# A step of Newton's method moved from VectorE to GpSimd in the second of four graph layers

## The chip, the cores and the metric

The kernel runs on one core of one Trainium2 chip. The metric is the device time of one execution in microseconds (us), as the median of several runs. Besides the timed runs there is one profiled execution, from which all views of the profile come.

## The reference

Four graph layers follow each other on 4096 nodes of 256 features, with one 4096 x 4096 adjacency matrix of 0 and 1. Each layer is `x = layernorm(x + layer(x, adj))`. The change sits in the second layer, an attention of four heads under a mask:

```python
def _layernorm(x, axis=-1, eps=1e-5):
    m = jnp.mean(x, axis=axis, keepdims=True)
    v = jnp.var(x, axis=axis, keepdims=True)
    return (x - m) / jnp.sqrt(v + eps)
...
q = _split_heads(x @ Wq + bq)
k = _split_heads(x @ Wk + bk)
v = _split_heads(x @ Wv + bv)
mask = (edge.T.astype(jnp.float32) - 1.0) * 10000.0
scores = jnp.einsum('hnd,hmd->hnm', q, k) / np.sqrt(HEAD_DIM)
scores = scores + mask[None, :, :]
attn = jax.nn.softmax(scores, axis=-1)
ctx = jnp.einsum('hnm,hmd->hnd', attn, v)
```

What matters here is the layer norm at the end: for every node one value `1 / sqrt(v + eps)` is needed.

## The kernel before, in words

All features stay in SBUF, in the tile `X` (128 partitions, 32 tiles of nodes, 257 columns). Every layer works on blocks of 512 nodes, eight blocks in all, which are the columns of a tile of scores; for each block it goes over all 4096 nodes on the other side.

In the second layer (`multi_head_attention`) that other side is cut into 64 half tiles of 64 nodes. A unit is a pair of a block `b` and a half tile `j`, and there are 512 units. For each unit:

- `scores` (line 622) puts the products of keys and queries of all four heads into a PSUM tile `p`, of which there are three; ScalarE takes the exponential in place (line 624).
- `weights` (line 634) multiplies on VectorE by the mask into an SBUF tile `prob`, of which there are eight.
- The row sums of `prob` are gathered for the softmax in three slots of the tile `den`: for even `j` GpSimd adds `prob` into slot 0 (line 641; for `j` = 0 a copy, line 639); for odd `j` a DMA issued by GpSimd adds `prob` into slot 1 or 2 in turn (line 647; the first two of a block are plain DMAs of the SP queue, line 645).
- `sums` (line 655) multiplies `prob` with the values on TensorE, three units behind `scores` (`LAG = 3`).

While a block runs, the block before it is finished piece by piece by `finish(b - 1, j)`: the slots of `den` are joined on VectorE (line 664), the sums and results are turned on TensorE (lines 677 to 692), divided and added to `X` (lines 706 and 709). Mean and variance of four tiles of nodes follow at `j` = 21 to 27 (lines 125 and 126). At `j` = 29 `begin_root` adds `eps` on VectorE (line 151), and ScalarE computes a first value of the inverse root as `exp(-0.5 * ln(v))` (lines 130 and 131). `end_root` makes it exact by one step of Newton's method, four instructions on 128x4 numbers (lines 137 to 140), at `j` = 33. At `j` = 35, 37, 39 and 41 `scale_row` (line 155) writes the normalised rows. `finish` is called with the `j` that is three behind the unit whose `scores` and `weights` were just written, so that its instructions stand behind `weights` of `j` + 3.

The order on an engine is settled in two ways. In this loop it is written out by hand for TensorE, VectorE and ScalarE:

```python
fixed = {mybir.EngineType.PE, mybir.EngineType.DVE, mybir.EngineType.Activation}
with tc.manual_schedule(engines=fixed):
```

These three keep the order of the program. The order on GpSimd and on the SP queue is chosen by the framework's planner, from dependencies, its own costs, and the order of the program as priority. In the third layer only TensorE's order is by hand, in the fourth none. Waits between engines are added by the framework.

Of the kernel before, what the change touches and what calls it, by code (L numbers as in the profile page):

```python
# [14 lines left out]
OP = mybir.AluOpType  # L15
# [13 lines left out]
def kernel(  # L29
# [27 lines left out]
    nc = tc.nc  # L57
# [65 lines left out]
    def one_row(mv, k, y):  # L123
        st = fin.tile([P, 6], FP, name="bn")
        nc.vector.bn_stats(st, y)
        nc.vector.bn_aggr(mv[:, k, :], st)
# [4 lines left out]
        nc.scalar.activation(r, r, AF.Exp, scale=-0.5)  # L131
        return r

    def end_root(v, r, n):

        s = fin.tile([P, n], FP, name=f"s{n}")
        nc.vector.tensor_tensor(s, r, r, OP.mult)
        nc.vector.tensor_tensor(s, s, v, OP.mult)
        nc.vector.tensor_scalar(s, s, -0.5, 1.5, OP.mult, OP.add)  # L139
        nc.vector.tensor_tensor(r, r, s, OP.mult)  # L140

    def inverse_root(v, n):

        r = first_root(v, n)
        end_root(v, r, n)
        return r

    def begin_root(mv):
        n = mv.shape[1]
        v = fin.tile([P, n], FP, name=f"v{n}")  # L150
        nc.vector.tensor_scalar_add(v, mv[:, :, 1], EPS)
        return v, first_root(v, n), n

    def scale_row(y, mv, r, k):
        nc.vector.tensor_scalar(y, y, mv[:, k, 0:1], r[:, k:k + 1], OP.subtract, OP.mult)

    def normalise(ys, mv):
        v, r, n = begin_root(mv)
        end_root(v, r, n)
        for k, y in enumerate(ys):  # L160
            scale_row(y, mv, r, k)
# [35 lines left out]
    def additive_heads(a, H, slope, early, narrow, ahead):  # L197
# [7 lines left out]
        with ExitStack() as lay:  # L205
# [92 lines left out]
            def finish(b, j):  # L298

                if j in (4, 10):  # L300
                    k = (j - 4) // 3
                    pos[b, k], pos[b, k + 1] = turned(bank, b, k), turned(bank, b, k + 1)
                    if k == 0 and b + 2 < NB:
                        rows(b + 2, pos[b, 0][:, HC + 1, :])
                if j in (4, 7, 10, 13):
                    k = (j - 4) // 3
                    outputs(pos[b, k], b, k)
                elif j == 15:
                    roots[b] = begin_root(mvs[b])
                elif j == 18:  # L310
                    end_root(*roots[b])
                elif j in (19, 21, 23, 25):
                    k = (j - 19) // 2
                    scale_row(X[:, b * QB + k, :D], mvs[b], roots[b][1], k)
# [194 lines left out]
    def multi_head_attention(w_sb, b_sb, tail, rows_of_den, narrow_edges):  # L509
# [11 lines left out]
        kept, den, rden, mvs, roots = {}, {}, {}, {}, {}  # L521
        with ExitStack() as lay:
# [140 lines left out]
            def join_sums(b, n, eng=nc.vector):  # L663
                eng.tensor_tensor(den[b][:, 0, :], den[b][:, 0, :], den[b][:, n, :], OP.add)

            def row_sums(bank, b):


                kept[b].append(fin1.tile([P, QW], FP, name=f"kept{KC}"))
                pds = [bank() for _ in range(KC)]  # L670
                for r in range(KC):
                    for s in range(2):
                        for c in range(KC):
                            g = 2 * r + s
                            half = slice(c * d, (c + 1) * d)
                            lo = r * QW + s * QW // 2
                            nc.tensor.matmul(pds[c][g * G:(g + 1) * G, :QW // 2], ones[half, :G],
                                             den[b][half, 0, lo:lo + QW // 2], start=True, stop=True)
                for c in range(KC):
                    nc.scalar.copy(kept[b][KC][:, c * QW // 2:(c + 1) * QW // 2], pds[c][:, :QW // 2])  # L680

            def turned_row_sums(bank, b):
                pd = bank()
                for k in range(QB):
                    nc.tensor.transpose(pd[:, k * P:(k + 1) * P], kept[b][KC][:, k * P:(k + 1) * P], ident)
                return pd

            def turned_half(bank, b, k):
                po = bank().rearrange("p (k f) -> p k f", f=D)
                for i in range(2):  # L690
                    for c in range(KC):
                        nc.tensor.transpose(po[:, i, c * P:(c + 1) * P],
                                            kept[b][c][:, (k + i) * P:(k + i + 1) * P], ident)
                return po

            def reciprocals(pd, b):
                rden[b] = fin.tile([P, QB, H], FP, name="rden4")
                parts = pd.rearrange("p (c k r s g) -> p k c r s g", c=KC, k=2, r=KC, s=2)
                for s in range(2):
                    nc.vector.reciprocal(rden[b][:, 2 * s:2 * s + 2, :].rearrange("p k (c r) -> p k c r", c=KC),  # L700
                                         parts[:, :, :, :, s, 0])

            def half(po, b, k):

                heads = po.rearrange("p k (h d) -> p (k h) d", h=H)
                nc.vector.tensor_tensor(heads, heads, rden[b][:, k:k + 2, :].rearrange("p k h -> p (k h)").unsqueeze(2)
                                        .to_broadcast([P, 2 * H, d]), OP.mult)
                y = X[:, b * QB + k:b * QB + k + 2, :D]
                nc.vector.tensor_tensor(y, po, y, OP.add)

            def halves():

                p = ps.tile([P, KC, QW], FP, name="p")
                left = [p[:, r, :] for r in range(KC)]
                return lambda: left.pop(0)

            def finish(b, j):

                rows = [X[:, b * QB + k, :D] for k in range(QB)]
                if j in (7, 9):  # L720
                    join_sums(b, j // 2 - 2)
                elif j == 12:
                    row_sums(halves(), b)
                elif j == 15:
                    bank = halves()
                    pd = turned_row_sums(bank, b)
                    po = turned_half(bank, b, 0)
                    reciprocals(pd, b)
                    half(po, b, 0)
                elif j == 18:  # L730
                    half(turned_half(halves(), b, 2), b, 2)
                elif j in (21, 23, 25, 27):
                    k = (j - 21) // 2
                    if k == 0:
                        mvs[b] = fin.tile([P, QB, 2], FP, name="mv")
                    one_row(mvs[b], k, rows[k])
                elif j == 29:
                    roots[b] = begin_root(mvs[b])
                elif j == 33:
                    end_root(*roots[b])  # L740
                elif j in (35, 37, 39, 41):
                    k = (j - 35) // 2
                    scale_row(rows[k], mvs[b], roots[b][1], k)
# [6 lines left out]
            with tc.manual_schedule(engines=fixed):  # L750
                for i in range(len(units) + LAG):
                    b, j = units[i - LAG] if i >= LAG else (-1, 0)
                    if i < len(units):
                        scores(*units[i])
                    if j == NH - 1:
                        sums(b, j)
                    if i < len(units):
                        weights(*units[i])
                    if b >= 0 and j < NH - 1:
                        sums(b, j)  # L760
                    if b > 0:
                        finish(b - 1, j)
# [238 lines left out]
```

## Time and profile before

| What | Value |
|---|---|
| Median of 3 runs | 2920.45 us (2920.34 to 2920.62) |
| Profiled execution, its own time | 2920.01 us |
| Its span, first to last instruction | 2918.1 us |
| Granted TensorE clock | 0.999 |
| Busy: TensorE, VectorE, ScalarE, GpSimd | 2901.0, 1959.0, 1668.3, 927.0 us |
| Second layer's loop | from about 815 to 1723 us of the span |
| In it: busy TensorE, VectorE, ScalarE, GpSimd | 902.4, 705.2, 566.7, 802.2 us of 908 us |

PE is TensorE's matmul, PEld its load of weights, DVE is VectorE, ACT is ScalarE, POOL is GpSimd, SP is SyncE. L139 is line 139 of the kernel. [...] An arrow in brackets names what ended an idle time.

### The profile page before, as it was taken

Reading aid. Unit: us, or ns where it says so; the run is one execution under the profiler, and the core shown is the slowest. Engines: PE = TensorE matmul, PEld = TensorE weight load, DVE = VectorE, ACT = ScalarE, POOL = GpSimd, SP = SyncE. Lnnn points to the kernel's source line nnn. Section 1 sums busy time; section 2 is a strip of 40 time slices with the busy share of each in tenths; the row PEclk is TensorE's granted clock in tenths of the full one; section 3 lists DMA queues with packets and bytes.
Section 4 is the critical chain, followed back from the end, with each engine's and each line's share of the span. In section 5 each row is a group of like instructions: output and inputs, shape, how many; then the busy total and the mean of one; then the engine's idle time right before and its main releaser. Section 6 shows DMA issues by size and latency. Waiting matters only on the chain.

```text
span 2918.1 us, 50377 instructions
## 1 busy us (share of the span) xinstructions
PE 2901.0 (99%) x20269; PEld 1564.5 (54%) x20269; DVE 1959.0 (67%) x2545; ACT 1668.3 (57%) x2613; POOL 927.0 (32%) x647
## 2 busy tenths in 40 slices
PE   9999999999999999999999999999999999999998
PEld 5333333333643333333333358888888777777776
DVE  8899999997677877877877765555655323333333
ACT  7899999997356666666666654444454222222222
POOL 0010010100068888988889860000000000000000
PEclk9999999999999999999999999999999999999999
DMA  7566666664068888889889874444442333333331
GB/s 204 107 135 140 136 140 142 135 134 84 1 142 191 182 187 189 181 186 191 180 189 188 184 164 138 153 152 150 154 136 60 49 58 58 58 58 58 58 58 29
DMA packets 207148, 374.94 MB, mean 128 GB/s; under 512 B 15057, under 2 KB 90817, under 8 KB 206018
## 3 DMA queue, kind: packets, MB, share of 16 engines
q0 software_dynamic: 102304, 177.77, 38.5%
q1 hardware_dynamic: 104336, 193.69, 20.2%
q8 instruction: 159, 2.61, 0.3%
q14 instruction: 75, 0.61, 0.1%
q10 hardware_dynamic: 274, 0.26, 0.0%
HBM read 317.07 MB, written 21.04 MB: 116 GB/s over the span
## 4 chain that ended last, share of the span: by engine, by line
PE 97%; DVE 2%; ACT 0%; issue 0%; DMA 0%; DVEq 0%; SPq 0%
PE acc L274 23%; PE acc L875 15%; PE p L622 15%; PE acc L655 14%; PE acc L440 8%; PE g L440 8%; PE p L864 4%; PE g L864 3%; PE g L550 2%; PE g L177 1%; PE pv L564 1%; PE g L118 1%; PE acc L823 1%; PE acc L177 1%; DVE prob L634 1%; DVE s L139 1%
## 5 line engine op out<-in xcount | busy, mean ns | idle before, releaser
L634 DVE TENSOR_TENSOR prob<-p,mask 128x1024 f32<-128x1024 f32 x512 | 623.0, 1223 | 197.2 <-ACT p L624 193.4
L624 ACT ACTIVATE p<-p,shift 128x1024 f32<-128x1024 f32 x512 | 556.2, 1088 | 331.9 <-PE p L622 331.0
L274 PE MATMUL acc<-prob,V 128*32 128x512 f32 x6144 | 664.0, 592 | 1.2 <-DVE prob L264 1.2
L641 POOL TENSOR_TENSOR den<-den,prob 128x1024 f32<-128x1024 f32 x248 | 618.8, 2495 | 72.4 <-DVE prob L634 62.9
L261 ACT ACTIVATE prob<-row,dst 128x512 f32<-128x512 f32 x1020 | 633.2, 712 | 0.1
L264 DVE SCALAR_TENSOR_TENSOR prob<-prob,mask 128x2048 f32<-128x2048 f32 x256 | 582.7, 2288 | 24.1 <-ACT prob L261 20.4
L622 PE MATMUL p<-qT,kT 64*64 64x512 f32 x4096 | 532.7, 590 | 5.6 <-DVE prob L634 5.6
L655 PE MATMUL acc<-prob,V 64*64 64x512 f32 x4096 | 531.5, 589 | 0.0
L875 PE MATMUL acc<-X,prob 128*128 128x257 f32 x2048 | 485.2, 380 | 0.0
L875 PEld LDWEIGHTS acc<-X,prob 128*128 128x128 f32 x2048 | 388.5, 190 | 160.7 <-issue 113.4
L868 DVE TENSOR_TENSOR prob<-prob,mask 128x512 f32<-128x512 f32 x256 | 176.5, 691 | 418.8 <-ACT prob L867 417.6
L274 PEld LDWEIGHTS acc<-prob,V 128*32 128x32 f32 x6144 | 197.3, 110 | 453.1 <-issue 434.2
L91 POOL COPY tick<-prob 128x1 f32<-128x1 f32 x35 | 39.8, 1136 | 1017.5 <-DVE prob L264 644.3
L432 ACT ACTIVATE e<-row,dst 128x512 f32<-128x512 f32 x256 | 184.2, 722 | 235.1 <-DVE prob L434 209.0
L655 PEld LDWEIGHTS acc<-prob,V 64*64 64x64 f32 x4096 | 155.9, 133 | 285.3 <-issue 278.1
L622 PEld LDWEIGHTS p<-qT,kT 64*64 64x64 f32 x4096 | 153.7, 133 | 284.4 <-issue 255.7
L434 DVE SCALAR_TENSOR_TENSOR prob<-e,mask 128x512 f32<-128x512 f32 x256 | 178.5, 698 | 185.7 <-PE acc L440 94.5
L808 POOL DMA_DIRECT2D mask<-in_adjT x64 | 47.5, 743 | 633.8 <-DVE prob L868 509.7
L647 POOL DMA_DIRECT2D den<-prob x240 | 225.9, 941 | 28.0 <-DVE prob L634 21.0
L867 ACT ACTIVATE prob<-p 128x512 f32<-128x512 f32 x144 | 85.8, 596 | 260.1 <-PE p L864 246.0
L440 PE MATMUL g<-V,prob 128*128 128x257 f32 x1024 | 225.6, 380 | 0.0
L440 PE MATMUL acc<-V,prob 128*128 128x257 f32 x1024 | 225.1, 380 | 0.0
(154 smaller groups left out, 1972.2 us busy)
## 6 DMA issues: line engine op xcount, KB each, us to landing
mask<-in_adjT SPq DMA_DIRECT2D x256, 512.0 KB
den<-prob POOLq DMA_DIRECT2D x240, 512.0 KB, 5.3
mask<-edges SPq DMA_DIRECT2D x256, 128.0 KB
mask<-in_adjT POOLq DMA_DIRECT2D x64, 512.0 KB, 5.6
edges<-in_adj POOLq DMA_DIRECT2D x32, 512.0 KB, 9.8
den<-prob SPq DMA_DIRECT2D x16, 512.0 KB
row<-far SPq DMA_DIRECT2D x7, 1024.0 KB
X<-in_x SPq DMA_DIRECT2D x7, 512.0 KB
```

The costliest lines, as they stand in the source:

```text
L261: nc.scalar.activation(z[:, h, :], r, AF.Relu, bias=-1.0, scale=dst[:, j, h:h + 1])
L264: nc.vector.scalar_tensor_tensor(z, z, 1.0, mask[m][:, j % MJ, :].unsqueeze(1).to_broadcast([P, H, QW]), OP.add, OP.mult)
L274: nc.tensor.matmul(acc[b][h * G:(h + 1) * G, n, :], part, prob[b, j][:, h, :], start=(j == 0), stop=(j == NT - 1))
L440: nc.tensor.matmul(acc[b][k][:, :D + 1], prob[b, j][:, k * P:(k + 1) * P], V[:, j, :], start=(j == 0), stop=(j == NT - 1))
L622: nc.tensor.matmul(p[c * d:(c + 1) * d, r, :], kT[half, c, j * d:(j + 1) * d], qT[half, c, cols], start=True, stop=True)
L624: nc.scalar.activation(p, p, AF.Exp, bias=shift)
L634: nc.vector.tensor_tensor(z, p, mask[m][:, j % MJ, :].unsqueeze(1).to_broadcast([P, KC, QW]), OP.mult)
L641: nc.gpsimd.tensor_tensor(to, to, flat, OP.add)
L647: nc.gpsimd.dma_start(to, flat, accum_op=OP.add)
L655: nc.tensor.matmul(acc[b][c][r * d:(r + 1) * d, :], V[half, j, r * d:(r + 1) * d], prob[b, j][half, r, :], start=(j == 0), stop=(j == NH - 1))
L864: nc.tensor.matmul(p, T[:, 0, j * P:(j + 1) * P], T[:, 1, cols], start=True, stop=True)
L875: nc.tensor.matmul(acc[b][k], prob[b, j][:, k * P:(k + 1) * P], X[:, j, :], start=(j == 0), stop=(j == NT - 1))
```

## The change

In the second layer's `finish`, the four instructions of `end_root` are issued on GpSimd rather than on VectorE, and at half tile 31 of the running block rather than at 33. `end_root` gets the engine as an argument; its other callers keep VectorE. `begin_root` stays at 29, `scale_row` at 35 to 41.

```diff
-    def end_root(v, r, n):
+    def end_root(v, r, n, eng=nc.vector):
 
         s = fin.tile([P, n], FP, name=f"s{n}")
-        nc.vector.tensor_tensor(s, r, r, OP.mult)
-        nc.vector.tensor_tensor(s, s, v, OP.mult)
-        nc.vector.tensor_scalar(s, s, -0.5, 1.5, OP.mult, OP.add)
-        nc.vector.tensor_tensor(r, r, s, OP.mult)
+        eng.tensor_tensor(s, r, r, OP.mult)
+        eng.tensor_tensor(s, s, v, OP.mult)
+        eng.tensor_scalar(s, s, -0.5, 1.5, OP.mult, OP.add)
+        eng.tensor_tensor(r, r, s, OP.mult)
...
                 elif j == 29:
                     roots[b] = begin_root(mvs[b])
-                elif j == 33:
-                    end_root(*roots[b])
+                elif j == 31:
+
+                    end_root(*roots[b], nc.gpsimd)
                 elif j in (35, 37, 39, 41):
```

## The prediction

> **What bounds the kernel now.** I read the page's chain that ended last first. It says that the whole program is a stream of matmuls:
>
> ```profile
> PE 97%; DVE 2%; ACT 0%; issue 0%; DMA 0%; DVEq 0%; SPq 0%
> ```
>
> So only what opens a gap on TensorE (PE) costs time, and a step on VectorE (DVE) or GpSimd (POOL) counts only where it makes PE late. Next, the waits of the second layer alone (815 to 1725 us). Columns: who waited on whom, total us, times, longest.
>
> ```profile
> PE p L622 <- DVE prob L634: 5.6, 8, 0.8
> POOL den L641 <- DVE prob L634: 62.9, 121, 3.1
> ```
>
> PE waits eight times here: once at the layer's start (819 us), and seven times for a late product of line 634. The loop calls `finish(b - 1, j)` in seven blocks, so that is once per block. The chain in order of time shows what made line 634 late (start us, length us):
>
> ```profile
> 1216.34 0.90 PE p L622 x8
> ...
> 1218.44 1.22 DVE prob L634
> ...
> 1219.97 2.54 DVE s L139
> ...
> 1222.61 1.23 DVE prob L634
> ...
> 1223.89 1.09 PE p L622 x8
> ```
>
> Line 139 is one instruction of the very step that the change moves, on 128x4 numbers. The two answers for line 139 (layer two and the boundary after it, then the first layer; min/median/max ns) show how odd its 2.5 us are:
>
> ```profile
> L139 DVE TENSOR_SCALAR s<-s x8: 170/2528/2528, 992.6 to 1761.0; 128x4 f32<-128x4 f32 x8
> L139 DVE TENSOR_SCALAR s<-s x8: 170/170/171, 183.1 to 745.7; 128x4 f32<-128x4 f32 x8
> ```
>
> The same instruction costs 0.17 us where GpSimd isn't adding. In layer two it costs 2.51 to 2.53 us in all seven blocks. The timeline gives the reason:
>
> ```profile
> 1216.87 2.36 POOL L641 TENSOR_TENSOR den<-den,prob 128x1024 f32<-128x1024 f32 x1
> ...
> 1219.19 0.87 POOL L647 DMA_DIRECT2D den<-prob  x1
> ...
> 1219.82 2.63 POOL L641 TENSOR_TENSOR den<-den,prob 128x1024 f32<-128x1024 f32 x1
> ...
> 1219.97 2.53 DVE L139 TENSOR_SCALAR s<-s 128x4 f32<-128x4 f32 x1
> 1222.53 0.16 DVE L140 TENSOR_TENSOR r<-r,s 128x4 f32<-128x4 f32 x1
> 1222.61 2.35 DVE L634 TENSOR_TENSOR prob<-p,mask 128x1024 f32<-128x1024 f32 x2
> ...
> 1224.13 0.87 POOL L647 DMA_DIRECT2D den<-prob  x1 [1.67 <-DVE prob L634]
> ```
>
> GpSimd's add starts at 1219.82, line 139 at 1219.97; the add ends at 1222.45, line 139 at 1222.50. The small instruction sits out the whole add. Line 634 of the next half tile waits behind it, and both PE and GpSimd (1.67 us idle) wait for that.
>
> [...] The trace agrees: line 139 ends 0.05 us after the add. It also shows what isn't held: line 155, a TENSOR_SCALAR whose scalars come from SBUF, stays at 404 to 424 ns everywhere, and line 634 (one input in PSUM) at about 1.22 us beside running adds.
>
> **The cost of the stall.** The timeline of PE alternates lines 622 and 655 every 0.858 us. Around the stall the starts are 1222.17, 1223.89, 1224.80, 1225.65: three steps take 3.48 us in place of 3 x 0.858 = 2.575 us. The loss is 0.905 us; the other six blocks show the same 1.71 or 1.72 us step. Seven blocks: 7 x 0.905 = **6.3 us**. PE loses less than DVE: the product of half tile 37 starts at 1222.61, while its undisturbed place is 1218.44 + 1.717 = 1220.16, so it is 2.45 us late. PE thus had 2.45 - 0.905 = 1.55 us of cushion.
>
> **The change part by part.**
>
> *Removed from DVE:* lines 137 to 140 at half tile 33 of the finished block. They come when half tile 36 of the running block is on DVE (the loop runs three ahead); I call the times by that count. From 1219.58 to 1222.61 they hold DVE 3.03 us per block; the line 634 that follows goes back to 1220.16. Worth 0.905 us of PE per block. Nothing else on PE waits for line 634 in these blocks, so I name no next late thing.
>
> *Unchanged:* line 151 and the two ACT instructions of `begin_root`, at half tile 32. ACT's wait there (1.42 us) costs PE nothing now and will not then. Their result is there at 1213.35.
>
> *Added to POOL:* four instructions on 128x4, in program order after the add of half tile 34 (1216.87 to 1219.2) and ahead of the DMA issue of half tile 35. No trace row has such an instruction. The nearest is the tick copy on one element a partition:
>
> ```profile
> L91 POOL COPY tick<-prob x35: 185/314/2519, 31.7 to 2186.0; 128x1 f32<-128x1 f32 x35
> ```
>
> Below, 0.185 us each; above, its mean of 1.136 us. The long ones belong to the first layer, beside line 264, a 2.29 us DVE instruction with both inputs in SBUF, and none such runs at half tile 34. [...] I take 0.3 us each, 1.2 us in all (0.74 to 4.5).
>
> *Moved past:* the DMA issue of half tile 35 goes from 1219.19 to 1220.4, the add of 36 from 1219.82 to about 1221.0. That add ends at about 1223.4, where today the next issue starts at 1224.13: the 1.67 us idle pays for the 1.2 us. The issue lands 5.3 us later (median), at 1225.7; its source buffer is wanted again eight half tiles on, by line 634 of 43 at about 1220.16 + 6 x 1.717 = 1230.5; and the next addition into the same slot is issued at 39, near 1227. Both are covered, and with 4.5 us (landing at 1229.0) the buffer still is. SP's queue isn't passed, and no DMA is added. Cost to PE: none.
>
> *Added wait:* line 155 on DVE (half tile 38, after line 634 ends at 1221.88 + 1.22 = 1223.1) now waits for POOL. The roots are ready at 1219.2 + 1.2 = 1220.4, 2.7 us before. At 1.136 us each they come at 1223.7; DVE waits 0.6 us, and line 634 of half tile 39, queued behind, is late by about that, within the cushion of 1.55. So the price doesn't touch PE up to (1223.1 + 1.55 - 1219.2) / 4 = 1.36 us each.
>
> **Sum:** 2920.01 - 6.3 = 2913.7 us for the profiled execution (span 2918.1 and 1.9 around it). The median of the runs is 0.44 above it, so **2914.1 us**, 0.22% faster. A measurement of this kernel can tell about 0.2% (5.8 us) from no change, so the whole gain just reaches it.
>
> **The rivals.**
>
> *Dear instructions (same).* If each costs 1.5 us with the hand-over between dependent ones, the roots come at 1225.2, DVE waits 2.1, PE loses 2.1 - 1.55 = 0.55 per block: 7 x (0.905 - 0.55) = 2.5 gained, 2918 us. [...] Against: the two starts on POOL in the first microsecond, a fill of `ident` and the select on it, lie 0.28 us apart.
>
> *POOL's queue (slower).* Line 749 fixes the order of PE, DVE and ACT alone; POOL's is the planner's. If it puts the four behind the add of half tile 38, that add waits for 1223.1, ends near 1225.5, and the roots come at 1226.7. DVE waits 3.6, PE loses 3.6 - 1.55 = 2.05 per block: 7 x (2.05 - 0.905) = 8 us slower, 2928 us. Behind the add of 36 they come at about 1223.4 and cost nothing, so it decides between 36 and 38. For: nothing ties the four to place. Against: POOL's adds and issues stand in program order today, and where the planner orders DVE too (1760 us) lines 137 to 140 stand together.
>
> *The stall stays (same).* If the lock is not the cause, or another DVE instruction meets it, 2920. Against: the seven identical lock-outs, and that none of lines 155, 125 and 634 beside an add is long.
>
> *The planner moves later work (either way).* Layers three and four leave DVE and ACT to it; moved times could change orders there by some us, 2911 to 2918.
>
> **How the numbers follow.** Forecast 0.70, dear 0.07, queue 0.09, stays 0.06, later work 0.08. Of the forecast I count a seventh as ending just inside 0.2%. Faster: 0.60 + 0.06 of the last rival = 0.66. Slower: 0.09. Same: the rest, 0.25. The forecast's own range is 2913.2 to 2915; to hold eight in ten it reaches up over the dear case, 2918, and down to 2912.8 for a little from later work.
>
> **What would show it.** Right: no line 139 on DVE in layer two; four small POOL instructions once per block, together, about 1.2 us; PE's step of 1.72 us gone, the total of PE waiting for line 634 down from 5.6 to about 0.8; DVE not waiting ahead of line 155; the block's period 113.70 - 0.9 = 112.8 us. Wrong: an idle time on DVE ended by POOL, or a block of 113.7 us.

## The result and the profile after

The changed kernel takes 2913.39 us (median of 13 runs, 2912.29 to 2914.40); the kernel before took 2920.01 us in the runs beside it (13 runs, 2918.88 to 2920.95). That is 6.6 us less, a ratio of 0.9978 (95% interval 0.9969 to 0.9986). The forecast was 6.3 us less.

The profiled execution went from 2920.01 to 2912.32 us, 7.7 us less. To see where, read the first and last start of a line that opens and closes the second layer: the answer for line 622 on PE (min/median/max ns, first and last start in us). First before, then after:

```profile
L622 PE MATMUL p<-qT,kT x4096: 589/589/640, 815.7 to 1718.7; 64*64 64x512 f32 x196
```

```profile
L622 PE MATMUL p<-qT,kT x4096: 589/589/640, 814.5 to 1711.1; 64*64 64x512 f32 x196
```

The stretch shrinks from 903.0 to 896.6 us, by 6.4. The other 1.2 us lie ahead of the layer, where the two kernels do the same; behind it nothing was gained or lost by more than 0.3 us (line 875, now 876, last starts at 2909.7 and 2902.4). So the layer is the place to compare kernels in, and I call 896.6 and 903.0 the *length of the stretch* below.

In the page's chain of the changed kernel VectorE has 1% in place of 2%, and of PE's waits for line 634 in the second layer only the one at the layer's start is left:

```profile
PE 99%; DVE 1%; ACT 0%; DMA 0%; issue 0%; SPq 0%; DVEq 0%
```

```profile
PE p L622 <- DVE prob L634: 0.8, 1, 0.8
```

The timeline of the changed kernel shows GpSimd and the two VectorE instructions that hand over to and take from it (start us, length us):

```profile
1209.76 0.16 DVE L151 TENSOR_SCALAR v<-mv 128x4 f32<-128x4 f32 x1
1210.00 2.36 POOL L641 TENSOR_TENSOR den<-den,prob 128x1024 f32<-128x1024 f32 x1
...
1212.33 0.19 POOL L137 TENSOR_TENSOR s<-r 128x4 f32<-128x4 f32 x1
1212.60 0.20 POOL L138 TENSOR_TENSOR s<-s,v 128x4 f32<-128x4 f32 x1
1212.89 0.19 POOL L139 TENSOR_SCALAR s<-s 128x4 f32<-128x4 f32 x1
...
1213.16 0.20 POOL L140 TENSOR_TENSOR r<-r,s 128x4 f32<-128x4 f32 x1
1213.63 0.88 POOL L647 DMA_DIRECT2D den<-prob  x1 [0.27 <-issue]
...
1220.07 0.41 DVE L155 TENSOR_SCALAR X<-X,mv,r 128x256 f32<-128x256 f32 x1
```

The four start 0.27 to 0.29 us apart and hold back the next DMA issue to 1.30 us after the first of them. They stand behind the add of half tile 32, the first one after line 151, not behind that of 34. The roots are there at 1213.4, 6.7 us before line 155 wants them.

### The profile page after: what moved, and what is told of

Same layout as the page of the kernel before. It is cut to its first block, busy times and chain, and to the rows that moved or that the text cites. A ratio compares the mean times of both kernels' runs of the same rounds, so it can differ in the third digit from the quotient of the medians.

```text
span 2910.5 us, 50377 instructions
## 1 busy us (share of the span) xinstructions
PE 2898.3 (100%) x20269; PEld 1564.1 (54%) x20269; DVE 1940.4 (67%) x2517; ACT 1668.1 (57%) x2613; POOL 932.3 (32%) x675
## 4 chain that ended last, share of the span: by engine, by line
PE 99%; DVE 1%; ACT 0%; DMA 0%; issue 0%; SPq 0%; DVEq 0%
PE acc L274 23%; PE acc L876 15%; PE acc L655 15%; PE p L622 15%; PE g L440 8%; PE acc L440 8%; PE p L865 4%; PE g L865 3%; PE g L550 2%; PE g L177 1%; PE pv L564 1%; PE g L118 1%; PE acc L824 1%; PE acc L177 1%; PE g L286 0%; PE p L692 0%
## 5 line engine op out<-in xcount | busy, mean ns | idle before, releaser
L641 POOL TENSOR_TENSOR den<-den,prob 128x1024 f32<-128x1024 f32 x248 | 628.6, 2535 | 71.3 <-DVE prob L634 64.4
L647 POOL DMA_DIRECT2D den<-prob x240 | 233.4, 972 | 15.8 <-DVE prob L634 7.5
```

The source lines that it names most:

```text
L641: nc.gpsimd.tensor_tensor(to, to, flat, OP.add)
L647: nc.gpsimd.dma_start(to, flat, accum_op=OP.add)
```

## The experiments

All ratios are against the kernel before, in the same session on the same chip.

### e1: the half tile alone

```diff
-                elif j == 33:
+                elif j == 31:
                     end_root(*roots[b])
```

> The four instructions stay on VectorE and only move from half tile 33 to 31, so that they stand behind line 634 of half tile 34, which ends when GpSimd starts its add of the same half tile. Lock theory: line 139 sits out that add as well, DVE is some 2.6 us late for half tile 35, the cushion of 1.55 us takes part of it and PE loses about 1.1 us in each of seven blocks: 1.4 us more than before, about 2921.5 (2920 to 2923), line 139 again near 2 us or more. Rival, the slot is what pays and the engine only goes along: 2913.5, line 139 at 0.17 us.

Measured: 2921.52 us, ratio 1.0006 (0.9997 to 1.0014); the stretch is 904.4 us, 1.4 longer than before. Line 139 in this kernel:

```profile
L139 DVE TENSOR_SCALAR s<-s x7: 2236/2241/2241, 990.2 to 1673.5; 128x4 f32<-128x4 f32 x7
```

It sits out the add of half tile 34 in place of that of 36: in one block the add runs from 1217.81 to 1220.16, line 139 from 1217.95 to 1220.19. "Lock" in the recorded texts is to be read as this hold, an instruction on VectorE that ends only when the add does (0.03 us after it here). The earlier half tile brings nothing on VectorE; that the medians show 1.3 us more is what was forecast, but the interval does not tell it from no change.

### e2: another form of line 139

```diff
-    def end_root(v, r, n):
+    halves_ = const.tile([P, 2], FP, name="nwt")
+    nc.vector.memset(halves_[:, :1], -0.5)
+    nc.vector.memset(halves_[:, 1:], 1.5)
+
+    def end_root(v, r, n, minus=-0.5, plus=1.5):
...
-        nc.vector.tensor_scalar(s, s, -0.5, 1.5, OP.mult, OP.add)
+        nc.vector.tensor_scalar(s, s, minus, plus, OP.mult, OP.add)
...
-                    end_root(*roots[b])
+                    end_root(*roots[b], halves_[:, :1], halves_[:, 1:])
```

> As before (VectorE, half tile 33), but line 139 of the second layer takes its two constants from SBUF, one per partition, as line 155 does, so that it is no longer a form which the add holds up. Rival A, [...]line 139 falls to 0.17 us, nothing takes its place, the gain is the change's own, 2913.5. My theory, with a lock that also holds an instruction with two SBUF inputs beside a GpSimd instruction that reads SBUF: line 139 falls to 0.17 us, but line 140 (two SBUF inputs), right behind it, sits out the rest of the add at 2.2 to 2.4 us, and the time stays at 2920 (2919 to 2921).

Measured: 2919.96 us, ratio 0.9999 (0.9991 to 1.0007), as I expected, but not for my reason. The timeline, where lines 141 to 144 are the four (143 is line 139 of before) and 645 is GpSimd's add:

```profile
1218.46 0.16 DVE L142 TENSOR_TENSOR s<-s,v 128x4 f32<-128x4 f32 x1
1218.52 2.60 POOL L645 TENSOR_TENSOR den<-den,prob 128x1024 f32<-128x1024 f32 x1
1218.66 2.49 DVE L143 TENSOR_SCALAR s<-s,nwt 128x4 f32<-128x4 f32 x1
1221.19 0.16 DVE L144 TENSOR_TENSOR r<-r,s 128x4 f32<-128x4 f32 x1
```

The instruction with its constants in SBUF is held just as long (2.49 us, 2.53 before), and the hold did not move to the line behind it (0.16 us). Line 155 has that form too, so the prediction's remark that it isn't held is in doubt. The probe below (e8) takes that up.

### e3: the four behind the add of half tile 38

```diff
-                        nc.gpsimd.tensor_tensor(to, to, flat, OP.add)
+                        added[b, j] = nc.gpsimd.tensor_tensor(to, to, flat, OP.add)
...
-                elif j == 31:
-                    end_root(*roots[b], nc.gpsimd)
                 elif j in (35, 37, 39, 41):
                     k = (j - 35) // 2
+                    if k == 0:
+                        seen = added[b + 1, 38]
+                        with tc.issue_after(getattr(seen, "ins", seen)):
+                            end_root(*roots[b], nc.gpsimd)
```

> The changed kernel with the four GpSimd instructions tied behind the add of half tile 38 of the running block (line 155 still stands behind line 634 of 38 on VectorE). Theory of the cushion: the add of 38 starts when its product is there, some 0.1 us after line 155 could start, takes 2.4 us, the four 1.1 us: line 155 waits 3.6 to 3.8 us, PE loses that less 1.55, about 2.1 to 2.2 per block, 7 x 2.15 = 15 us over the changed kernel: 2928 (2926 to 2931). Rival, PE has more slack than one block's reading showed: 2913 to 2920. Rival, no cushion: 7 x 3.7 = 26 us, 2939.

Measured: 2927.36 us, ratio 1.0026 (1.0016 to 1.0036): slower than before. The waits of the second layer (who, on whom: total us, times, longest):

```profile
DVE X L155 <- POOL r L140: 25.5, 7, 3.7
PE p L622 <- DVE prob L634: 12.9, 8, 1.8
```

VectorE waits 25.5 / 7 = 3.64 us per block. Against the changed kernel the time is 2927.36 - 2913.39 = 14.0 us longer, 2.00 per block. (The two were timed apart; the kernel before took 2920.23 us beside the one and 2920.01 beside the other.) The cushion, as an estimate from these two times, is thus 3.64 - 2.00 = 1.64 us, where the stall of before had given 1.55. The order is that of the prediction's slower rival, for which 2928 was forecast.

### e4: on VectorE, at half tile 34

```diff
-                elif j == 33:
+                elif j == 34:
                     end_root(*roots[b])
```

> The four stay on VectorE, at half tile 34, behind line 634 of 37. The add of 36 is then three quarters over: line 139 is held some 1 us, DVE is about 0.9 us late for half tile 38, within the cushion of 1.55. Lock and cushion theory: PE loses nothing, 2913.5 (2912.5 to 2915), without GpSimd. Rival, the gain needs the work off VectorE: 2920.

Measured: 2913.46 us, ratio 0.9977 (0.9969 to 0.9986), the changed kernel's time without GpSimd; the stretch is 896.6 us. The hold is still there, but falls on another line:

```profile
L137 DVE TENSOR_TENSOR s<-r x7: 1234/1244/1260, 994.4 to 1671.1; 128x4 f32<-128x4 f32 x7
```

The add was a little over half done when line 137, with two inputs in SBUF, met it (it runs from 1218.51 to 1221.13 in the block of the next sentence, and line 137 starts at 1219.93), where three quarters had been expected. The next line 634 starts at 1221.78 in one block, where 1218.79 + 1.717 = 1220.51 was its place: 1.27 us late, under the cushion, and PE shows no gap: its waits for line 634 come to the 0.8 us at the layer's start.

### e5: the add taken away from beside the step

```diff
-                if j % 2 == 0:
+                if j % 2 == (0 if j not in (36, 37) else 1):
```

> As before (the four on VectorE at half tile 33), but the parts of half tiles 36 and 37 in the row sums change places: 36 is added by a DMA, 37 by GpSimd. The same work, only no GpSimd add runs while the four are on VectorE. Theory, the running add is the cause: line 139 takes 0.17 us, the step of 1.72 us on PE is gone, and the time is that of the changed kernel, 2913.5 (2912.5 to 2915.5), though the four never leave VectorE. Rival, the four instructions themselves, or their place, make VectorE late: 2920.

Measured: 2915.04 us, ratio 0.9981 (0.9974 to 0.9989). The four stay on VectorE and the 2.5 us are gone, but line 155 now meets an add:

```profile
L139 DVE TENSOR_SCALAR s<-s x7: 170/170/171, 992.2 to 1670.8; 128x4 f32<-128x4 f32 x7
L155 DVE TENSOR_SCALAR X<-X,mv,r x28: 400/543/3214, 995.3 to 1684.1; 128x256 f32<-128x256 f32 x28
```

The add of 37 starts late, after a DMA that waited for an earlier one to land, and the first line 155 of each block meets it and ends with it (1223.55 in one block; the add ends at about 1223.5, an estimate, since the trace joins it with the next from 1220.70 to 1225.83, and that one is taken at the usual 2.36). In five of the seven blocks this line takes 1.7 to 1.8 us, within the cushion. In two it takes 3.0 and 3.2 us, past the cushion, and PE waits 2.2 us over the layer in place of 0.8. That is most of the 1.6 us by which this run misses the changed kernel. In these two blocks line 155 is recorded as starting 0.17 and 0.37 us ahead of the add; why it is held even so stays open. So the run shows both sides at once: without the running add the step costs nothing where it stood, and another instruction that meets an add pays for it.

It also shows that not just any work of GpSimd holds the step. A DMA issue runs beside it, and its lines take 0.15 to 0.17 us:

```profile
1217.87 0.87 POOL L647 DMA_DIRECT2D den<-prob  x1
...
1218.27 0.15 DVE L137 TENSOR_TENSOR s<-r 128x4 f32<-128x4 f32 x1
1218.46 0.16 DVE L138 TENSOR_TENSOR s<-s,v 128x4 f32<-128x4 f32 x1
1218.65 0.17 DVE L139 TENSOR_SCALAR s<-s 128x4 f32<-128x4 f32 x1
```

### e6: on GpSimd, at half tile 33

```diff
-                elif j == 31:
+                elif j == 33:
                     end_root(*roots[b], nc.gpsimd)
```

> The changed kernel with the call of the step at half tile 33, as it was before the change: only the engine changes. The planner puts the four at the same place of GpSimd's queue as for 31, behind the add of half tile 32. Theory: 2913.4 (2912.5 to 2914.5), the engine alone carries the change and the number 31 does nothing. Rival, the earlier half tile matters: over 2915.

Measured: 2913.12 us, ratio 0.9976 (0.9966 to 0.9985). Since the planner orders GpSimd's queue, the four stand in the same place for 31 and 33: line 137 starts 2.57 us after line 151 in the changed kernel and 2.56 here. The half tile in the change moves nothing.

### e7: behind the add of half tile 36

The edit is that of e3 with 36 in place of 38.

> As the run behind the add of half tile 38, but tied behind the add of 36. That add ends some 3.3 us after the product of 36 began, the four take 1.1 us, line 155 waits 0 to 0.6 us. Theory of the cushion: nothing of it reaches PE, 2913.5 (2912.5 to 2915). Rival, every wait of VectorE counts: 0.5 us in seven blocks, 2917.

Measured: 2913.43 us, ratio 0.9975 (0.9965 to 0.9984); the stretch is 896.6 us. VectorE does wait, 3.0 / 7 = 0.43 us per block, and nothing of it reaches PE:

```profile
DVE X L155 <- POOL r L140: 3.0, 7, 0.5
```

### e8: which VectorE instructions are held

```diff
+            few = keep.tile([P, 8], FP, name="few")
+            nc.vector.memset(few, 0.5)
+            to = keep.tile([P, D], FP, name="to")
+            st = keep.tile([P, 6], FP, name="st")
+
+            def probe(j, y):
+                if j == 44:
+                    nc.vector.tensor_scalar(to[:, :4], few[:, :4], -0.5, 1.5, OP.mult, OP.add)
+                elif j == 46:
+                    nc.vector.tensor_scalar(to[:, :4], few[:, :4], few[:, 6:7], few[:, 7:8], OP.mult, OP.add)
+                elif j == 48:
+                    nc.vector.tensor_tensor(to[:, :4], few[:, :4], few[:, :4], OP.mult)
+                elif j == 50:
+                    nc.vector.tensor_scalar(to, y, few[:, 6:7], few[:, 7:8], OP.subtract, OP.mult)
+                elif j == 52:
+                    nc.vector.bn_stats(st, y)
+                elif j == 54:
+                    nc.vector.tensor_scalar_add(to[:, :4], few.rearrange("p (k n) -> p k n", n=2)[:, :, 1], EPS)
+                elif j == 56:
+                    nc.vector.tensor_scalar(to[:, :3], few[:, :3], -0.5, 1.5, OP.mult, OP.add)
...
+                probe(j, rows[0])
```

> The changed kernel with seven VectorE instructions more per finished block, on scratch data that nothing reads, each behind line 634 of an odd half tile late in the block, when GpSimd's add has 0.5 to 1 us to go: which forms are held? Undisturbed they take about 0.17 us (128x4) or 0.41 us (128x256). My theory after line 139 was held in both of its forms and line 137 too: every form [...]is held, by 0.4 us and more: constants in the instruction 128x4, constants from SBUF 128x4, two SBUF inputs 128x4, and line 155's form 128x256, which in the profile before never met an add. Not held: the statistics of a row (one input). Open: a source with a stride of two, as line 151 has, and three elements in place of four. Rival: only the first three are held and line 155's form is not. The time is that of the changed kernel, 2913 to 2916, since each hold is under the cushion.

Measured: 2915.98 us in one run, so without an interval. The answers for the seven lines, in the order of the code (min/median/max ns):

```profile
L724 DVE TENSOR_SCALAR to<-few x7: 1000/1046/1764, 1012.8 to 1690.4; 128x4 f32<-128x4 f32 x7
L726 DVE TENSOR_SCALAR to<-few x7: 1227/1432/1485, 1016.7 to 1693.9; 128x4 f32<-128x4 f32 x7
L728 DVE TENSOR_TENSOR to<-few x7: 1446/1474/1480, 1020.4 to 1697.3; 128x4 f32<-128x4 f32 x7
L730 DVE TENSOR_SCALAR to<-X,few x7: 1602/1604/1609, 1024.0 to 1701.0; 128x256 f32<-128x256 f32 x7
L732 DVE BATCH_NORM_STATS2 st<-X x7: 410/410/412, 1027.8 to 1704.8; 128x6 f32<-128x256 f32 x7
L734 DVE TENSOR_SCALAR to<-few x7: 1829/2023/2114, 1030.4 to 1707.6; 128x4 f32<-128x4 f32 x7
L736 DVE TENSOR_SCALAR to<-few x7: 1476/1482/1489, 1034.7 to 1711.6; 128x3 f32<-128x3 f32 x7
```

The timeline of one block shows the three kinds beside their adds:

```profile
1245.18 2.35 POOL L641 TENSOR_TENSOR den<-den,prob 128x1024 f32<-128x1024 f32 x1 [0.50 <-DVE prob L634]
...
1246.08 1.48 DVE L728 TENSOR_TENSOR to<-few 128x4 f32<-128x4 f32 x1
...
1248.85 2.35 POOL L641 TENSOR_TENSOR den<-den,prob 128x1024 f32<-128x1024 f32 x1 [0.50 <-DVE prob L634]
...
1249.75 1.60 DVE L730 TENSOR_SCALAR to<-X,few 128x256 f32<-128x256 f32 x1
...
1252.64 2.35 POOL L641 TENSOR_TENSOR den<-den,prob 128x1024 f32<-128x1024 f32 x1 [0.62 <-DVE prob L634]
...
1253.54 0.41 DVE L732 BATCH_NORM_STATS2 st<-X 128x6 f32<-128x256 f32 x1
```

Line 728 starts 0.90 us into an add of 2.35 and ends at 1247.56, 0.03 us after it. Line 730, line 155's form, is held for about 1.2 us of its 1.60 (line 155 takes 0.41 undisturbed). The statistics, 0.90 us into the third add, take their usual 0.41. Every `tensor_scalar` on SBUF tried here is held (medians): with constants in the instruction (1.05 us) or in SBUF (1.43), with a stride (2.02), with three elements (1.48) in place of four, where lines 139 and 151 take 0.17 and 0.16 us undisturbed. So is the instruction with two SBUF inputs (1.47 us; line 137 takes 0.15 in e5). The row statistics are not (0.41 us), and line 634, whose other input is in PSUM, is not: it takes its 1.20 to 1.23 us beside the adds of the kernel before too.

## Why the prediction was right, point by point

- **The stall and its cause.** Right. Line 139 waited for a running GpSimd add: where no add runs beside it, it takes 0.17 us on VectorE too (e5), and in another form (e2, 2.49 us) or half tile (e1, 2.24 us) it is held again. Why an add holds it, no run here shows; the runs show which instructions wait, and until when (0.05 us after the add's end in the kernel before).
- **Seven times 0.905 us.** Right: 6.3 forecast, the stretch is 6.4 shorter, the medians differ by 6.6. From the starts of line 137, 986.8 to 1663.5 in six periods, a block takes 112.8 us, as forecast.
- **The cushion of 1.55 us.** Right in kind and size. Delays of 0.43 us (e7) and 1.27 us (e4) cost PE nothing; 3.64 us (e3) cost 2.00. The figures for the cushion itself, 1.55 and 1.64, are estimates.
- **The price on GpSimd.** 0.3 us each was taken, my estimate, within the 0.185 to 1.136 us that the tick copy allowed; 0.27 to 0.29 from start to start were measured. The rival with dear instructions was empty.
- **Their place in GpSimd's queue.** Wrong, and without effect on the sum. The prediction put them behind the add of half tile 34 in program order; the planner put them behind that of 32, as early as the roots allow, whatever the call says (e6). The rival that built on this freedom had the right threshold: behind 36 free (e7), behind 38 slower by 7.1 us (e3), 8 forecast.
- **The 1.67 us that GpSimd idles.** Wrong in its reasoning. This idle time was part of the stall: GpSimd waited for the late product of half tile 37. It goes with the stall, also where GpSimd has nothing added (in e4 the issue of 37 follows the add of 36 without it in six of seven blocks), so it could not pay for the four. They also stand earlier than forecast, 2.57 us after the start of line 151 in place of some 6.5 us. Counted from line 151, the adds of 34 and 36 start about 0.35 us later than before in most blocks. PE waits for none of this. The step's other argument, that the buffers and the slot are wanted only later, is the one that is left for it.
- **"What isn't held."** Wrong for line 155. Its 404 to 424 ns were read as proof that it passes beside an add. In the trace before it never started inside one with more than 0.05 us to go: it stands behind line 634 of an even half tile, at the end of one add and ahead of the next. The probe shows its form held (1.60 us in place of 0.41), and e5 the line itself (1.83 us in one block, with an add running). Whether its constants in SBUF are what count was not tried.

## What to carry to other kernels

A small VectorE instruction that takes many times its usual length (here 2.53 us in place of 0.17) is worth a look at what GpSimd runs at that moment: the cure can be another engine, but also one slot later (e4 gives the same gain without GpSimd, 2913.46 us) or moving the add (e5 gives most of it, 2915.04 us). Before calling an instruction free of such a hold, see in the timeline that it ever started inside the other's span; a min/max from instructions that never met proves nothing. And count a delay only past the cushion of the engine that sets the end: here VectorE could be late by 1.27 us once in a block and it cost nothing, and the limit is estimated at about 1.6 us.

## What the runs showed of the hardware that was not expected

A float32 `tensor_scalar` with per-partition constants from SBUF (128x4: 1.43 us, 128x256: 1.60 us) waits for a running GpSimd add just as one with its constants in the instruction does (128x4: 1.05 us in e8, 2.53 us in the kernel before), and so does one with a strided source (2.02 us) or three elements (1.48 us); undisturbed, line 139 (128x4, constants in the instruction) takes 0.17 us and line 155 (128x256) 0.41 us. Row statistics over 256 elements do not (0.41 us).
